# Self-attention of a transformer block: reciprocals two slots on between the maxima, second group transposed a slot later, values and projections a slot on, seven probability buffers

## The chip, the cores and the metric

The kernel runs on one core of one Trainium2 chip. The metric is the device time of one execution in microseconds (us); "before" is the median of three runs. A profile is one execution taken by the hardware profiler. In its rows PE is the matrix engine TensorE (PEld its weight loads), DVE is VectorE, ACT is ScalarE, POOL is GpSimd, and SP is the engine that issues nearly all of this kernel's DMAs. L504 is line 504 of the kernel.

## What is computed

One transformer block in float32 on x (2 x 1024 x 256) with a context (2 x 154 x 192): self-attention and cross-attention with 16 heads of 64, then a gated feed-forward layer of 1024. The reference, cut to its core:

```python
def _attention(xq, xkv, wq, wk, wv, wo, bo):
    q = (xq @ wq).reshape(B, S, N_HEADS, D_HEAD)
    k = (xkv @ wk).reshape(B, T, N_HEADS, D_HEAD)
    v = (xkv @ wv).reshape(B, T, N_HEADS, D_HEAD)
    attn = jnp.einsum('bihd,bjhd->bhij', q, k) * D_HEAD ** (-0.5)
    attn = jax.nn.softmax(attn, axis=-1)
    out = jnp.einsum('bhij,bjhd->bihd', attn, v).reshape(B, S, D_ATTN)
    return out @ wo + bo
h = _layernorm(x, ln1_g, ln1_b)
x = _attention(h, h, sa_wq, sa_wk, sa_wv, sa_wo, sa_bo) + x
h = _layernorm(x, ln2_g, ln2_b)
x = _attention(h, cond_emb, ca_wq, ca_wk, ca_wv, ca_wo, ca_bo) + x
h = _layernorm(x, ln3_g, ln3_b)
p = h @ ff_w1 + ff_b1
a, gate = (p[..., :D_FF], p[..., D_FF:])
return a * jax.nn.gelu(gate, approximate=False) @ ff_w2 + ff_b2 + x
```

## The kernel before

The order of all instructions is written out by hand (`tc.manual_schedule()`): each engine runs its own in the order in which the program issues them, and semaphores make it wait where data or a buffer isn't ready. What an engine has to do next is therefore stuck behind whatever it waits for.

**Units and slots.** A unit is a pair of heads of one batch (16 units). Self-attention has `SA` = 128 slots, eight per unit (`2 * SH`, `SH` = 4); in this text n is the slot's number within its unit, and a half is four slots, that is half of a unit's queries. A slot takes two groups of 64 queries for both heads. `LAG` is 2.

**One slot p, engine by engine.** PE computes the two groups' scores into two PSUM tiles `s` (`scores`, L493); with two such tiles, the first group of the next slot can only start when the exponentials have read the first tile, and the second likewise. The 1024 keys of a query are spread over two blocks of partitions, 512 each, so a row's softmax comes in two parts. DVE takes the negated maxima of a group over its part (L654), ACT the four exponentials with their sums (`exponents`, L504; two per group), into a probability tile `p` of which there are six buffers (`pp`). Then the two parts' maxima and sums, in the small tile `st`, are exchanged between partitions by four small DMAs on SP (`exchange`, L514). In the next slot `join` computes from them on POOL the differences `dd` (L522, L523), on ACT their exponentials `ee` (L525), on POOL `zz` and the denominators `den` (L527, L529). DVE takes the reciprocal `rd` (L600), and POOL scales the four probability parts by it (L604). One slot later DVE transposes both groups (`turn_groups`, L618) into `pT`, a tile for each half (two buffers). When the four slots of a half are all transposed, PE multiplies with the values in two parts (`self_values`, `weigh`, L539), and ACT copies the sum `po` to `o_sa` (L639).

**What fills PE beside scores and values.** Of the eight slots of a unit, four hold a part of `self_values` (n = 2, 3, 6, 7 before). In the other four `run_work` runs the next unit's projections `pq_sa`, `pk_sa` (L362) and `pv_sa` (L393), pieces of the output projection `py_sa` (L467, added to x by DVE at L474), transposes of a normalisation (`ph_ln`, L280) and products for cross-attention (`pk`, `pe`). The lists `work`, `side` and `outs` hold what is still to do. In the first half no values are ready, so its slots run projections.

**Order within a slot before:** scores and both maxima; four exponentials; `join` of slot p - 1; exchange of slot p; both transposes of slot p - 2; an addition to x if there is one; the reciprocal of slot p - 1 and its four scalings; POOL's addition of a bias from `later`; loads; PE's work. So on DVE the reciprocal of p - 1 is the last of slot p and stands ahead of the maxima of p + 1.

**SP's queue** holds the exchange of each slot, the weight loads of later units (`load_ahead`: queries at n = 2, keys at n = 3, values at n = 7), the swap of halves of `v_sa` (L409, L410, after the value projection), tiles of the second batch's x and chunks of `sa_wo` (`load_ahead_parts`).

**After slot 127** come 48 steps c of cross-attention (three per unit) that overlap with the last self-attention work, and then the feed-forward part.

Of the kernel before, what the change touches and what calls it, by code (L numbers as in the profile page):

```python
# [13 lines left out]
P = 128  # L14
# [4 lines left out]
def tile_transformer_block(ctx: ExitStack, tc: tile.TileContext, a: dict, out: bass.AP):  # L19
# [44 lines left out]
    pp_ = ctx.enter_context(tc.tile_pool(name="pp", bufs=6))  # L64
# [80 lines left out]
    def load_ahead_parts():  # L145

        wo["sa"] = const.tile([P, NPAIR, D], F32, tag="wo", name="sa_wo")  # L150
# [5 lines left out]
        def chunk(i):  # L156
            nc.sync.dma_start(out=wo["sa"][:, i, :], in_=w["sa_wo"][i * P:(i + 1) * P, :])

        tiles = [lambda t=t: tile_of_x(t) for t in tile_order("sa")]
        chunks = [lambda i=i: chunk(i) for i in range(NPAIR)]  # L160
# [300 lines left out]
    def out_piece(kind, b, g, t):  # L461
# [3 lines left out]
        for e in range(2):  # L465
            for i in range(HP):
                nc.tensor.matmul(  # L467
                    py[:, e * D:(e + 1) * D], lhsT=o[:, i, (t + e) * P:(t + e + 1) * P],
                    rhs=wo[kind][:, g * HP + i, :], start=(i == 0), stop=(i == HP - 1),
# [29 lines left out]

    def exponents(u, sc, st, i):  # L500
# [17 lines left out]
    def join(u, st):  # L518
# [4 lines left out]
        nc.gpsimd.tensor_scalar(dd, dd, 0.0, 1.0, op0=ALU.min, op1=ALU.mult)  # L523
        ee = small.tile([P, 2, 4], F32, tag="ee", name=f"ee_{u}")
# [24 lines left out]
    drain = []  # L549
# [42 lines left out]
    joins, groups, halves = [], [], {}  # L592

    def scale_groups(u, st, members):

        ee, den = join(u, st)

        def reciprocals():
            rd = small.tile([P, 4], F32, tag="rd", name=f"rd_{u}")
            nc.vector.reciprocal(rd, den)  # L600
            for i, pr in enumerate(members):
                for j in range(2):
                    c = 2 * i + j
                    nc.gpsimd.tensor_scalar(  # L604
                        pr[:, j, :], pr[:, j, :], rd[:, c:c + 1], ee[:, 0, c:c + 1],
                        op0=ALU.mult, op1=ALU.mult,
                    )
                groups.append(pr)

        return reciprocals  # L610

    def turn_groups(p):
        h, g = divmod(p, SH)
        if g == 0:
            halves[h] = pt_.tile([P, 2 * NK, QH // 2], F32, tag="pT", name=f"pT_{h}")
        for i in range(2):
            c = (2 * g + i) * KB
            nc.vector.transpose(  # L618
                halves[h][:, :, c:c + KB], groups.pop(0).rearrange("p j (n k) -> p (j n) k", k=KB)
            )  # L620
# [25 lines left out]
    def self_first(p):  # L646
# [6 lines left out]
        for i in range(2):  # L653
            nc.vector.tensor_reduce(st[:, 0, 0, i, :], sc[i], AX.X, ALU.max, negate=True)  # L654
# [32 lines left out]
    def load_ahead(p):  # L687
# [10 lines left out]
        if p == SA - 2:  # L698
            load_weights("ca", units[2][1], "q")
        if p == SH:  # L700
# [385 lines left out]
    with tc.manual_schedule():  # L1086
# [61 lines left out]
        for p in range(SA):  # L1148
# [7 lines left out]
            late = then()  # L1156
            if p >= LAG:
                turn_groups(p - LAG)
            if adds:
                adds.pop(0)()  # L1160
            if late:
                late()
            flush(kept)
            if later and (p < 4 or p % (2 * SH) in (2, 4, 6)):
# [4 lines left out]
            h, hg = divmod(p, SH)  # L1169
            if h == 0 or hg < LAG:  # L1170

                run_work(2 if p < SA - SH else 1, h % 2 or h == 0, sum_tile)
                if p == LAG:
                    load_weights("sa", units[1][1], "v")
                ui, n = divmod(p, 2 * SH)
# [163 lines left out]
```

## Time and profile before

| what | us |
|---|---|
| runs before | 1105.02, 1100.79, 1100.0; median 1100.79 |
| span of the profiled execution | 1100.3 |
| self-attention slots, first maxima of slot 0 to first cross scores | 18.8 to 713.4 |
| DVE's waits for `den` before the reciprocal (L600) | 34.9 in 43 waits |
| POOL's waits for the exchange before `dd` (L522) | 51.9 in 48 waits |
| ACT's waits for the maxima before the exponentials (L504) | 184.9 in 115 waits |

The profiled execution's own time is its span. A row of the timeline has the start in the span, the time of the merged instructions, engine, line, operation, tiles, count and, in brackets, the engine's idle time before it and what ended it. A row of the windows has the stretch, its length, the busy time of PE with the number of its instructions, TensorE's granted clock (1.00 is full), the DMA engines' share and GB/s. A row of the waits has the waiting engine and line, who ended the wait, total us, number and longest. A row of the DMA issues ends with the median time from issue to landing. Times of PE's matmuls overlap, and their ends are modelled, so starts are compared, not lengths.

### The profile page before, as it was taken

Reading aid. Unit: us, or ns where it says so; the run is one execution under the profiler, and the core shown is the slowest. Engines: PE = TensorE matmul, PEld = TensorE weight load, DVE = VectorE, ACT = ScalarE, POOL = GpSimd, SP = SyncE. Lnnn points to the kernel's source line nnn. Section 1 sums busy time; section 2 is a strip of 40 time slices with the busy share of each in tenths; the row PEclk is TensorE's granted clock in tenths of the full one; section 3 lists DMA queues with packets and bytes.
Section 4 is the critical chain, followed back from the end, with each engine's and each line's share of the span. In section 5 each row is a group of like instructions: output and inputs, shape, how many; then the busy total and the mean of one; then the engine's idle time right before and its main releaser. Section 6 shows DMA issues by size and latency. Waiting matters only on the chain.

```text
span 1100.3 us, 44912 instructions
## 1 busy us (share of the span) xinstructions
PE 1080.4 (98%) x18388; PEld 718.1 (65%) x18388; DVE 893.1 (81%) x1301; ACT 638.0 (58%) x2057; POOL 730.2 (66%) x1552
## 2 busy tenths in 40 slices
PE   8999999999999999999999999999999999899998
PEld 6556656556665565565665655567766677788887
DVE  5888999898989989999999989978877877644442
ACT  5666676667667656666776776666655554232221
POOL 2766777777777777677777777676756785555331
PEclk9999999999999999999999999999999999999999
DMA  3222112112111111111110111036765545000000
GB/s 93 67 61 52 45 40 57 39 46 52 25 42 43 29 42 32 39 42 24 42 42 14 42 33 28 20 82 159 179 155 123 117 106 114 1 10 10 15 15 29
DMA packets 104094, 60.71 MB, mean 55 GB/s; under 512 B 32330, under 2 KB 94674, under 8 KB 103890
## 3 DMA queue, kind: packets, MB, share of 16 engines
q1 hardware_dynamic: 102514, 57.07, 21.8%
q8 instruction: 145, 2.38, 0.9%
q10 hardware_dynamic: 1376, 0.79, 0.2%
q14 instruction: 59, 0.48, 0.1%
HBM read 27.91 MB, written 2.10 MB: 27 GB/s over the span
## 4 chain that ended last, share of the span: by engine, by line
PE 56%; ACT 12%; DVE 9%; DMA 8%; POOL 6%; SPq 5%; issue 4%; DVEq 0%; ACTq 0%; POOLq 0%
ACT p L504 11%; PE po L539 9%; PE s L493 9%; DVE st L654 6%; DMA st<-st 5%; PE pf L1069 5%; PE py_ca L467 5%; SPq L514 5%; PE poc L881 4%; PE pq_ca L362 4%; PE pb L1003 4%; PE py_sa L467 3%; PE sc L802 3%; PE pa L1003 2%; PE pc L1003 2%
## 5 line engine op out<-in xcount | busy, mean ns | idle before, releaser
L504 ACT ACTIVATE p<-s,st 128x512 f32<-128x512 f32 x512 | 345.3, 687 | 195.7 <-DVE st L654 184.9
L604 POOL TENSOR_SCALAR p<-p,rd,ee 128x512 f32<-128x512 f32 x512 | 385.7, 767 | 47.9 <-DVE rd L600 46.9
L654 DVE TENSOR_REDUCE st<-s 128x2 f32<-128x1024 f32 x256 | 300.7, 1216 | 23.7 <-PE s L493 9.4
L618 DVE STREAM_TRANSPOSE pT<-p 128x1024 f32<-128x1024 f32 x256 | 302.3, 1218 | 0.2 <-POOL p L604 0.2
L493 PE MATMUL s<-k_sa,q_sa 64*32 64x512 f32 x4096 | 261.0, 595 | 6.9 <-ACT p L504 6.0
L539 PE MATMUL po<-pT,v_sa 64*32 64x256 f32 x8192 | 239.8, 376 | 1.8 <-DVE pT L618 1.4
L539 PEld LDWEIGHTS po<-pT,v_sa 64*32 64x32 f32 x8192 | 174.9, 106 | 74.9 <-issue 22.0
L493 PEld LDWEIGHTS s<-k_sa,q_sa 64*32 64x32 f32 x4096 | 81.0, 106 | 111.6 <-ACT p L504 53.3
L818 ACT ACTIVATE p<-sc,neg 128x154 f32<-128x154 f32 x256 | 96.4, 407 | 82.9 <-DVE rden L826 79.7
L829 POOL TENSOR_SCALAR p<-p,rden 128x154 f32<-128x154 f32 x256 | 96.8, 398 | 56.9 <-DVE rden L826 56.5
L504 ACT ACTIVATION_READ_ACCUMULATOR p<-s,st 128x1 f32 x512 | 103.9, 203 | 0.0
L527 POOL TENSOR_TENSOR zz<-ee,st 128x8 f32<-128x8 f32 x128 | 25.9, 202 | 73.6 <-ACT ee L525 73.6
L393 PEld LDWEIGHTS pv_sa<-sa_wv,hT_ln 64*128 64x128 f32 x1024 | 58.5, 188 | 14.2 <-issue 7.5
L522 POOL TENSOR_TENSOR dd<-st 128x8 f32<-128x8 f32 x128 | 25.6, 200 | 55.5 <-DMA st<-st 51.9
L393 PE MATMUL pv_sa<-sa_wv,hT_ln 64*128 64x128 f32 x1024 | 61.7, 275 | 0.0
L467 PE MATMUL py_ca<-ca_wo,o_ca 128*128 128x256 f32 x256 | 60.0, 382 | 0.5 <-DVE o_ca L894 0.5
L467 PE MATMUL py_sa<-sa_wo,o_sa 128*128 128x256 f32 x256 | 59.7, 385 | 0.0
L467 PEld LDWEIGHTS py_sa<-sa_wo,o_sa 128*128 128x128 f32 x256 | 47.3, 190 | 17.8 <-ACT v_sa L402 6.7
L362 PE MATMUL pq_sa<-hT_ln,sa_wq 64*32 64x512 f32 (+1 forms) x976 | 58.8, 587 | 0.0
L362 PE MATMUL pq_ca<-hT_ln,ca_wq 64*128 64x512 f32 (+1 forms) x304 | 58.0, 589 | 0.0
L807 DVE TENSOR_REDUCE neg<-sc 128x6 f32<-128x924 f32 (+1 forms) x48 | 47.9, 999 | 12.1 <-PE sc L802 12.0
L362 PE MATMUL pk_sa<-hT_ln,sa_wk 64*32 64x512 f32 x960 | 57.4, 591 | 0.1
(117 smaller groups left out, 1462.9 us busy)
## 6 DMA issues: line engine op xcount, KB each, us to landing
wf<-pT_ca SPq DMA_DIRECT2D x128, 128.0 KB, 2.5
st<-st SPq DMA_DIRECT2D x512, 1.0 KB, 1.8
v_sa<-v_sa SPq DMA_DIRECT2D x32, 256.0 KB, 3.7
sa_wq<-in_L_xattn_sa_wq_dram SPq DMA_DIRECT2D x32, 128.0 KB, 3.2
sa_wk<-in_L_xattn_sa_wk_dram SPq DMA_DIRECT2D x32, 128.0 KB, 3.2
sa_wv<-in_L_xattn_sa_wv_dram SPq DMA_DIRECT2D x32, 128.0 KB, 3.0
ca_wq<-in_L_xattn_ca_wq_dram SPq DMA_DIRECT2D x32, 128.0 KB, 4.4
wf<-in_L_xattn_ff_w_dram SPq DMA_DIRECT2D x12, 256.0 KB, 3.9
```

What stands on the lines that cost most here:

```text
L362: nc.tensor.matmul(pq[r][f:f + m, at:at + n], lhsT=wt[own, c, f:f + m], rhs=h[own, c, t0:t0 + n], start=(c == 0), stop=(c == NH - 1), tile ...
L393: nc.tensor.matmul(pv[r][:, i * P:(i + 1) * P], lhsT=h[own, c, i * P:(i + 1) * P], rhs=wt[own, c, :], start=(c == 0), stop=(c == NH - 1), ...
L467: nc.tensor.matmul(py[:, e * D:(e + 1) * D], lhsT=o[:, i, (t + e) * P:(t + e + 1) * P], rhs=wo[kind][:, g * HP + i, :], start=(i == 0), st ...
L493: nc.tensor.matmul(sc[a4 * KB:(a4 + 1) * KB, j, :], lhsT=q[r, c:c + KB], rhs=k[r, h * HB:(h + 1) * HB], start=True, stop=True, tile_positi ...
L504: nc.scalar.activation(pr[:, j, :], sc[:, j, :], AF.Exp, bias=st[:, 0, 0, i, j:j + 1], accum_out=st[:, 0, 1, i, j:j + 1],)
L539: nc.tensor.matmul(po[a2][d:d + KB, :QH // 2], lhsT=v[r, t, e, d:d + KB], rhs=pT[r, d // DH * NK + n, :], start=(t == 0 and e == 0), stop= ...
L604: nc.gpsimd.tensor_scalar(pr[:, j, :], pr[:, j, :], rd[:, c:c + 1], ee[:, 0, c:c + 1], op0=ALU.mult, op1=ALU.mult,)
L618: nc.vector.transpose(halves[h][:, :, c:c + KB], groups.pop(0).rearrange("p j (n k) -> p (j n) k", k=KB))
L654: nc.vector.tensor_reduce(st[:, 0, 0, i, :], sc[i], AX.X, ALU.max, negate=True)
L818: nc.scalar.activation(pr_[:, j, i, :T], sc[:, j, i * T:(i + 1) * T], AF.Exp, bias=neg[:, j, i:i + 1], accum_out=den[:, j, i:i + 1],)
L829: nc.gpsimd.tensor_scalar(pr_[:, j, i, :T], pr_[:, j, i, :T], rden[:, j, i:i + 1], 1.0, op0=ALU.mult, op1=ALU.mult,)
L1003: nc.tensor.matmul(into[:, :BT], lhsT=lhs, rhs=wh[pair][i], start=first, stop=True, skip_group_check=True)
```

## The change

- The probability tiles get a seventh buffer. The room comes from the output weights: instead of one tile with all of `sa_wo` (later `ca_wo`), `load_out` loads the 256 KB for two head pairs into one of two buffers, again for each batch; for self-attention at n = 6 of every second unit, for cross-attention in the third step of every second unit.
- `join` is split into `differences` (`dd`) and `denominators` (`ee`, `zz`, `den`). POOL's order in slot p is now: two scalings of group 0 of p - 2, `dd` of p - 1, two scalings of group 1 of p - 2, `zz` and `den` of p - 1.
- The reciprocal of slot p - 2 stands between the two maxima of slot p.
- DVE then transposes group 1 of slot p - 3 and group 0 of slot p - 2.
- The values of a half start one slot later (n = 3, 4 and 7, 0), the other work moves to n = 1, 2, 5, 6, and in the first unit work runs in slots 0 to 6.
- The tail follows: the last half but one finishes its values in the first cross step, and the last reciprocals, scalings and transposes stand in cross steps 0 to 2.
- The tiles of the second batch's x are loaded in units 1 and 2.

```diff
-    pp_ = ctx.enter_context(tc.tile_pool(name="pp", bufs=6))
+    pp_ = ctx.enter_context(tc.tile_pool(name="pp", bufs=7))
...
-        pieces = tiles[:4] + chunks[:HP] + tiles[4:] + chunks[HP:]
-        slots = [u * 2 * SH + n for u in range(1, 5) for n in (0, 1, 4, 5)]
-        return dict(zip(slots, pieces))
+        slots = [u * 2 * SH + n for u in range(1, 3) for n in (0, 1, 4, 5)]
+        return dict(zip(slots, tiles))
+
+    def load_out(kind, b, g):
+
+        t = wo[kind, b, g] = p2.tile([P, HP, D], F32, tag="wo", name=f"{kind}_wo{b}_{g}")
+        c0 = g * HP * P
+        nc.sync.dma_start(
+            out=t, in_=w[f"{kind}_wo"][c0:c0 + HP * P, :].rearrange("(i p) d -> p i d", p=P))
...
+    def reciprocals(p):
+
+        v = slot[p]
+        v["rd"] = small.tile([P, 4], F32, tag="rd", name=f"rd_{p}")
+        nc.vector.reciprocal(v["rd"], v["den"])
+
+    def weighted(p, i):
+
+        v = slot[p]
+        pr = v["members"][i]
+        for j in range(2):
+            c = 2 * i + j
+            nc.gpsimd.tensor_scalar(
+                pr[:, j, :], pr[:, j, :], v["rd"][:, c:c + 1], v["ee"][:, 0, c:c + 1],
+                op0=ALU.mult, op1=ALU.mult,
+            )
...
+    def softmax_steps(p):
+
+        before, older = slot.get(p - 1), slot.get(p - 2)
+        if older:
+            weighted(p - 2, 0)
+        if before:
+            before["dd"] = differences(p - 1, before["st"])
+        if older:
+            weighted(p - 2, 1)
+
+    def softmax_join(p):
+
+        if p in slot:
+            v = slot[p]
+            v["ee"], v["den"] = denominators(p, v["st"], v["dd"])
...
-        for i in range(2):
-            nc.vector.tensor_reduce(st[:, 0, 0, i, :], sc[i], AX.X, ALU.max, negate=True)
+        maxima(sc[0], st, 0)
+        if p >= 2:
+            reciprocals(p - 2)
+        maxima(sc[1], st, 1)

         def then():
-            members = [exponents(f"{p}_{i}", sc[i], st, i) for i in range(2)]
-            late = scale_groups(*joins.pop(0)) if joins else None
+            members = [exponents(f"{p}_0", sc[0], st, 0)]
+            softmax_steps(p)
+            members.append(exponents(f"{p}_1", sc[1], st, 1))
+            softmax_join(p - 1)
             exchange(st)
-            joins.append((p, st, members))
-            return late
+            slot[p] = {"st": st, "members": members}
+            turn_group(p - 3, 1)
+            if p >= 2:
+                turn_group(p - 2, 0)
...
+        if n == 2 * SH - 2 and ui % HP == 1:
+            k = ui // HP
+            load_out("sa", *divmod(k, NQ))
...
-            if h == 0 or hg < LAG:
+            if p < 2 * SH - 1 or p % SH in (1, 2):

-                run_work(2 if p < SA - SH else 1, h % 2 or h == 0, sum_tile)
+                run_work(2 if p < SA - SH else 1, n > SH or p < SH, sum_tile)
...
             else:
-                run(lambda: self_values(h - 1, hg - LAG))
+                run(lambda: self_values(p // SH - 1 - (p % SH == 0), int(p % SH == 0)))
...
-            if c == 1:
-                turn_groups(SA - 2)
-            flush(drain)
+            if c < 2:
+                reciprocals(SA + c - 2)
             flush(lates)
+            if c < 3:
+                softmax_steps(SA + c)
+                if c == 0:
+                    softmax_join(SA - 1)
+                turn_group(SA + c - 3, 1)
+                if c < 2:
+                    turn_group(SA + c - 2, 0)
             lates.append(then())
...
-            if c == 1:
+            if c == 0:
+                run(lambda: self_values(2 * NU - 2, 1))
+            elif c == 1:
                 run(lambda: cross_queries(*nxt))
...
-                elif ui == HP:
-                    wo["ca"] = const.tile([P, NPAIR, D], F32, tag="wo", name="ca_wo")
-                    later[:0] = [lambda i=i: nc.sync.dma_start(
-                        out=wo["ca"][:, i, :], in_=w["ca_wo"][i * P:(i + 1) * P, :])
-                        for i in range(NPAIR)]
+                elif ui > HP and ui % HP == 1:
+                    load_out("ca", *divmod(ui // HP - 1, NQ))
...
+            if k == 0:
+                load_out("ca", B - 1, NQ - 1)
```

More of the change, by code (lines that the diff above doesn't have):

```diff
@@ L1155, in tile_transformer_block @@
             flush(stores)
-            late = then()
-            if p >= LAG:
-                turn_groups(p - LAG)
+            then()
             if adds:
                 adds.pop(0)()
-            if late:
-                late()
             flush(kept)
-            if later and (p < 4 or p % (2 * SH) in (2, 4, 6)):
+            ui, n = divmod(p, 2 * SH)
+            if later and (p < 4 or n in (2, 4, 6)):
                 later.pop(0)()
```

60 lines of the change are left out of this document (22 added, 38 removed).

## The prediction

> **What bounds the kernel now.** I read the page's busy shares first, then the time of whole head pairs on TensorE, then single slots engine by engine.
>
> ```profile
> PE 1080.4 (98%) x18388; PEld 718.1 (65%) x18388; DVE 893.1 (81%) x1301; ACT 638.0 (58%) x2057; POOL 730.2 (66%) x1552
> 60.25:671.29 611.04, 606.03 (x13748) 1.00 0.17 39
> 369.39:411.56 42.17, 42.17 (x985) 1.00 0.16 35
> 628.54:671.29 42.75, 42.75 (x988) 1.00 0.14 31
> L747 PE MATMUL pe<-ca_wv,ctxT 96*32 96x192 f32 (+1 forms) x48 | 2.4, 314 | 0.0
> 321.49 1.92 PE L493 MATMUL s<-k_sa,q_sa 64*32 64x512 f32 x32
> 323.21 3.66 PE L539 MATMUL po<-pT,v_sa 64*32 64x256 f32 x128
> 326.66 1.92 PE L493 MATMUL s<-k_sa,q_sa 64*32 64x512 f32 x32
> ```
>
> The three stretches begin where the scores of a unit's first slot begin: the first covers units 1 to 14, the others units 8 and 14, in which PE never stands; unit 14 has four normalisation transposes more, 0.58. In the last three rows a slot is 1.72 us of scores (321.49 to 323.21) and 3.45 of values (323.21 to 326.66): 5.17 us without a gap. So PE is the bound wherever it isn't held up, and the question is how often it is. Fourteen units at 42.17 are 590.4 us; the transposes, in eight of them by the program, add 4.6 and the products for `ends` 2.4. That makes 597.4 against 611.0: **PE loses 13.6 us in these 112 slots.** That is the ceiling for what the steady part of the change can give.
>
> Where it is lost shows in a slot with a late exchange, beside a quiet one:
>
> ```profile
> 333.34 2.35 DVE L654 TENSOR_REDUCE st<-s 128x2 f32<-128x1024 f32 x2
> 335.61 2.36 DVE L618 STREAM_TRANSPOSE pT<-p 128x1024 f32<-128x1024 f32 x2
> 338.08 0.18 DVE L600 RECIPROCAL rd<-den 128x4 f32<-128x4 f32 x1
> 338.38 1.23 DVE L654 TENSOR_REDUCE st<-s 128x2 f32<-128x1024 f32 x1
> 334.60 0.69 ACT L504 ACTIVATE p<-s,st 128x512 f32<-128x512 f32 x1 [1.18 <-DVE st L654]
> 337.27 0.22 ACT L525 ACTIVATE ee<-dd 128x8 f32<-128x8 f32 x1
> 333.32 3.01 POOL L604 TENSOR_SCALAR p<-p,rd,ee 128x512 f32<-128x512 f32 x4 [0.32 <-DVE rd L600]
> 336.30 0.20 POOL L522 TENSOR_TENSOR dd<-st 128x8 f32<-128x8 f32 x1
> 336.59 0.25 POOL L523 TENSOR_SCALAR dd<-dd 128x8 f32<-128x8 f32 x1
> 337.57 0.20 POOL L527 TENSOR_TENSOR zz<-ee,st 128x8 f32<-128x8 f32 x1 [0.73 <-ACT ee L525]
> 337.85 0.20 POOL L529 TENSOR_TENSOR den<-zz 128x4 f32<-128x4 f32 x1
> ```
>
> ```profile
> 204.62 2.35 DVE L654 TENSOR_REDUCE st<-s 128x2 f32<-128x1024 f32 x2
> 209.70 3.66 PE L539 MATMUL po<-pT,v_sa 64*32 64x256 f32 x128
> 213.64 1.09 PE L493 MATMUL s<-k_sa,q_sa 64*32 64x512 f32 x16 [0.27 <-ACT p L504]
> 216.00 3.84 PE L393 MATMUL pv_sa<-sa_wv,hT_ln 64*128 64x128 f32 x64
> 209.20 0.20 POOL L522 TENSOR_TENSOR dd<-st 128x8 f32<-128x8 f32 x1 [1.59 <-DMA st<-st]
> 210.57 0.18 DVE L600 RECIPROCAL rd<-den 128x4 f32<-128x4 f32 x1 [1.33 <-POOL den L529]
> DVE rd L600 <- POOL den L529: 34.9, 43, 3.1
> POOL dd L522 <- DMA st<-st: 51.9, 48, 13.9
> ```
>
> In the quiet slot the chain maxima, four exponentials, `ee`, `zz`, `den`, reciprocal fills 333.34 to 338.08, and the next maxima start at 338.38: 5.04 us, only 0.13 below PE's 5.17. DVE therefore pays back a delay at 0.13 us a slot. In the late slot `dd` waits for the exchange until 209.20, the reciprocal follows 1.37 later, and all of DVE has stood for 1.33. PE pays: values to scores take 3.94 instead of 3.45, and the scores 2.36 (213.64 to 216.00) instead of 1.72, 1.1 us together. The last two rows count such waits.
>
> **Part by part: the reciprocal.** It goes from the end of slot p+1 to between the maxima of slot p+2; 128 before and after, so no work is added. In time after a slot's first maximum, from the quiet slot: reciprocal at 1.14 (half of 333.34 to 335.61), the first two scalings 0.28 later (338.08 to 338.36 is the same step; the row at 333.32 is its predecessor) for 1.50 (half of 3.01), `dd` at 2.92 or when the exchange lands, 0.54 for its two operations, 1.50 for the other two scalings, 0.48 for `zz` and `den`: 5.44. Its reader stands at 5.17 + 1.14 = 6.31. So `dd` may start up to 3.75 before DVE is held; now it is 3.50 (5.17 less 0.30 less 1.37). But the second maximum now stands behind the reciprocal (0.18), so the second pair of exponentials, and with it the exchange, comes about 0.17 later. **The tolerance to a late exchange grows by 0.1 us only.** What is queued behind the waiting reciprocal is the second maximum and both transposes; for the maximum waits ACT's second pair, for that PE's next scores. What does improve is the pay-back:
>
> ```profile
> 317.55 2.36 DVE L654 TENSOR_REDUCE st<-s 128x2 f32<-128x1024 f32 x2 [1.35 <-DMA st<-st]
> 319.82 2.36 DVE L618 STREAM_TRANSPOSE pT<-p 128x1024 f32<-128x1024 f32 x2
> 322.11 0.66 DVE L474 TENSOR_TENSOR x<-py_sa,x 128x512 f32<-128x512 f32 x1
> 322.68 0.16 DVE L600 RECIPROCAL rd<-den 128x4 f32<-128x4 f32 x1
> 322.76 1.19 DVE L654 TENSOR_REDUCE st<-s 128x2 f32<-128x1024 f32 x1
> ```
>
> Where the reciprocal is ready, DVE's own slot is 2.27 + 2.29 + 0.08, or 4.64, up to 4.86 with a gap of 0.3 around the reciprocal: 0.3 to 0.5 us a slot against PE, not 0.13. The waits (43 in 128 slots) then mostly meet a DVE that has caught up. PE's slack for the second pair of exponentials: they end 3.93 after the maximum, at 326.69 in the slot of 322.76, and are needed at 326.66 + 0.86 = 327.52, so 0.83 now and 0.66 after. A stall of 1.33 less 0.1 less 0.66 leaves 0.57 of the 1.1 it costs now, and smaller ones less than that share. I take 8 of the 13.6 us as won. Bounds: 0 (tolerance all but unchanged, every wait still paid) and 13.6 (none paid).
>
> **Second transposition, scaling around `dd`, seventh buffer.** The second group's scaling ends at 4.96 and its transposition waits until the next slot: no wait. The first group's scaling ends at 2.92, its transposition stands at about 3.6: covered by 0.7; without it that much a slot. The exponentials reuse buffers whose transposition came a slot earlier, which needs seven; with six the second would wait inside its slot. Nothing, and POOL's bias additions now stand behind `den` and delay no `dd`: that is in the 8.
>
> **Values and projections a slot later.** Both move together, so each half's transposes still end a slot ahead of PE's use. But slot 6 has no large work for PE, since the first half's values begin in slot 7:
>
> ```profile
> 692.31:697.40 5.09, 3.38 (x52) 1.00 0.11 29
> 697.40:700.80 3.40, 3.40 (x33) 0.50 0.02 1
> 725.61 3.69 PE L539 MATMUL po<-pT,v_sa 64*32 64x256 f32 x128 [1.40 <-DVE pT L618]
> ```
>
> The 3.45 us of values that slot 6 has now move out of it. The next scores still wait for slot 6's exponentials: 1.27 from scores to maximum (321.49 to 322.76), 4.1 to the last exponential, 0.1 and 0.86 for the second group, 6.33 against 6.89 now. PE stands 3.45 - 0.56 = 2.9 us (2.4 to 3.45). The same happened once already: at 692.31 PE stood 1.7 of 5.09 us, and the clock was 0.50 for the next 3.40. I add 1.7 for that (0 to 3.4): **fill +4.6.** [...]
>
> At the end the moved half of values runs behind the first cross scores; it is the work that left slot 6, so only idle time counts. PE's wait of 1.40 for the last transpose becomes about 1.9, because that transpose now stands behind a slot's cross scalings on POOL: +0.5 (0 to 2.2, with a slow clock). The two slots without PE work near 695 get shorter by DVE's faster slot: -0.5 (0 to -0.9).
>
> **Loads.** Tiles of x come earlier; `sa_wo` and `ca_wo` come as 256 KB for each two head pairs, reloaded for each batch. On SP the self loads stand behind a slot's exchange, one in sixteen slots, eight slots ahead of their use, and the 16 chunks of 128 KB go. The halves of `v_sa` stand one slot later, still ahead of one exchange a unit. I take 0 (-1 to +2). The cross loads are a rival below.
>
> **Sum:** -8 + 4.6 + 0.5 - 0.5 = -3.4 on a span of 1100.3, so 1096.9; the median of the runs, 1100.79, lies 0.5 above the span: **1097.4**, within 0.5% (5.5 us, what counts here as no change).
>
> **Rivals.**
> (B) *All stalls paid back, clock kept at the fill.* -13.6 + 2.9 + 0.5 - 0.5 = -10.7: 1090.1. For it: the faster DVE, and unit 8 shows that 42.17 can be held. Against: the exchange's landing doesn't change.
> (C) *PE isn't the bound, and slots fall to the next loop.*
>
> ```profile
> 203.66 2.41 SPq L514 DMA_DIRECT2D st<-st  x4
> st<-st SPq DMA_DIRECT2D x512, 1.0 KB, 1.8
> ```
>
> A reciprocal depends on the one two slots before it: 0.16 to the second maximum, 2.6 to the end of its exponentials, 4.2 for the exchange (its four issues and a landing), 2.5 from `dd` to `den`; 9.5 for two slots, 4.75 for one, much like DVE's own 4.64 to 4.86. At 4.8 the 128 slots would take 0.37 less each beside the 10.7: 1043. [...] Against: PE's rows join without a gap at 5.17, and nothing in the diff shortens them.
> (D) *Slower: the exchange loop decides.* The threshold of `dd` has hardly moved, and a held reciprocal now delays the second exponentials, which have 0.66 of slack, not 0.83. From a `dd` start of about 3.6 us after the maximum (209.20 less 204.62, 4.58, in the late slot) each wait is paid as before and 0.17 more. None of the 13.6 is won, half of 43 waits cost 0.17 more (3.7), with fill and tail: +4.6 + 0.5 - 0.5 + 3.7 = +8.3, so 1109. Against: DVE's spare time.
> (E) *Cross attention waits for `ca_wo`*, so that the change doesn't do only what it says:
>
> ```profile
> 760.64 1.08 SPq L1256 DMA_DIRECT2D ca_wo<-in_L_xattn_ca_wo_dram  x2
> 768.14 1.89 PE L467 MATMUL py_ca<-ca_wo,o_ca 128*128 128x256 f32 x8
> wf<-in_L_xattn_ff_w_dram SPq DMA_DIRECT2D x12, 256.0 KB, 3.9
> ```
>
> A load of 256 KB takes 3.9, and some 7 us lie between issue and use. If SP is held 4 us, PE waits about 1 us for each of eight: -3.4 + 8 = +4.6, 1105.
>
> **Chances.** Forecast 0.46 (its own range 1093 to 1102), B 0.23, C 0.02, D 0.19, E 0.10. Faster by over 0.5% (below 1095.3): B, C and a quarter of the forecast, 0.36. Slower (above 1106.3): two thirds of D and a third of E, 0.16. The same: 0.48. The range 1088 to 1107 leaves out C, a fifth of B and over half of D, just under 0.2.
>
> **What would show it.** Right: DVE's waits before the reciprocal fall from 34.9 us to under 15 while those of `dd` on the exchange stay near 50; units 1 to 14 shrink by about 8 us to near 603; PE stands some 3 us behind the scores of slot 6 and the clock is 0.5 there; ACT's second pair starts later after the first. Wrong: a unit below 42 us (then PE wasn't the bound), reciprocal waits that stay, or PE waiting at the cross projections for `ca_wo`.

## The result and the profile after

The kernel after takes 1094.87 us (median of 9 runs, 1093.61 to 1099.67), the kernel before 1100.51 us (9 runs beside it, 1100.0 to 1105.02). The ratio is 0.9949, 95% interval 0.9936 to 0.9963: 5.6 us faster. The profiled execution after has a span of 1091.8 and took 1093.61; in all nine runs the time lies 1.8 us above the span.

First the page after: the busy shares, and the chain of work that ended last, by engine; the last row is that chain before.

```profile
PE 1070.7 (98%) x18388; PEld 703.4 (64%) x18388; DVE 881.2 (81%) x1301; ACT 643.5 (59%) x2057; POOL 729.9 (67%) x1552
PE 89%; DVE 3%; POOL 3%; ACT 2%; DMA 2%; SPq 1%; issue 1%; ACTq 0%; DVEq 0%; POOLq 0%
PE 56%; ACT 12%; DVE 9%; DMA 8%; POOL 6%; SPq 5%; issue 4%; DVEq 0%; ACTq 0%; POOLq 0%
```

The instruction counts are those of before. In the chain before, TensorE had 56%; the rest ran through ScalarE, VectorE, transfers and GpSimd. Now 89% of the chain is TensorE itself. Units 1 to 14, from the first scores of slot 8 to those of slot 120, and unit 14 alone, in the windows view after:

```profile
61.33:659.19 597.86, 597.80 (x13748) 354.37 (x13740) 547.43 (x625) 411.01 (x1203) 448.66 (x931) 1.00 0.18 42
616.45:659.19 42.74, 42.74 (x988) 24.89 (x980) 38.71 (x43) 29.18 (x89) 30.49 (x65) 1.00 0.15 33
```

611.04 us have become 597.86, with the same 13748 matmuls. The prediction worked out 597.4 for TensorE's own work there. The loss of 13.6 us has become 0.5. Unit 14, which had no gap before (42.75), is unchanged: TensorE is the bound now, and nothing in it became shorter. The waits (total us, times, longest):

```profile
POOL dd L526 <- DMA st<-st: 65.5, 62, 14.4
DVE rd L605 <- POOL den L537: 12.4, 19, 3.3
PE s L493 <- ACT p L508: 4.2, 6, 2.1
```

GpSimd waits for the exchange more often than before (62 times against 48). The exchanges came hardly earlier: in the mean of slots 8 to 121 `dd` starts 4.64 us behind the end of the exponentials, against 4.72 before. The reciprocal waits less (12.4 us against 34.9, 19 times against 43), and the waits that are left hardly reach TensorE. A late exchange in the timeline after: `dd` stands in slot 16, the reciprocal that needs it in slot 17 (start, duration, engine, instruction):

```profile
109.03 0.20 POOL L526 TENSOR_TENSOR dd<-st 128x8 f32<-128x8 f32 x1 [1.44 <-DMA st<-st]
109.55 1.52 POOL L613 TENSOR_SCALAR p<-p,rd,ee 128x512 f32<-128x512 f32 x2
109.82 1.23 DVE L502 TENSOR_REDUCE st<-s 128x2 f32<-128x1024 f32 x1 [0.47 <-ACT ee L533]
111.32 0.20 POOL L537 TENSOR_TENSOR den<-zz 128x4 f32<-128x4 f32 x1
111.56 0.18 DVE L605 RECIPROCAL rd<-den 128x4 f32<-128x4 f32 x1 [0.51 <-POOL den L537]
111.65 1.20 DVE L502 TENSOR_REDUCE st<-s 128x2 f32<-128x1024 f32 x1
112.88 0.69 ACT L508 ACTIVATE p<-s,st 128x512 f32<-128x512 f32 x1 [0.35 <-DVE st L502]
108.59 1.92 PE L493 MATMUL s<-k_sa,q_sa 64*32 64x512 f32 x32
110.31 3.64 PE L362 MATMUL pq_sa<-hT_ln,sa_wq 64*32 64x512 f32 x64
113.74 1.92 PE L493 MATMUL s<-k_sa,q_sa 64*32 64x512 f32 x32
```

`dd` starts 4.38 us after its slot's first maximum (104.65). That is nearly as late as in the late slot that the prediction showed (4.58), where VectorE stood 1.33 us and TensorE paid 1.1. Here the reciprocal waits 0.51, the second maximum with it, and ScalarE's second pair waits 0.35. TensorE's scores follow after 5.15 us (108.59 to 113.74) without a gap.

Where the time went, from the starts of the same instructions in both timelines:

| stretch | before | after | difference |
|---|---|---|---|
| first maximum of slot 0 to that of slot 8 | 44.19 | 43.66 | -0.53 |
| slot 8 to slot 120 (units 1 to 14) | 609.59 | 597.89 | -11.70 |
| slot 120 to slot 127 | 38.10 | 35.97 | -2.13 |
| slot 127 to the end of the last self values | 23.23 | 30.15 | +6.92 |
| to the first cross output projection | 34.25 | 34.52 | +0.27 |
| to the first product of the feed-forward's second weight | 201.45 | 200.01 | -1.44 |
| to the end | 130.69 | 130.70 | 0.01 |

The first and the fourth stretch belong together, since 3.45 us of values moved from the one to the other. The sum, with 0.11 at the start, is -8.49, while the medians differ by 5.6. The two profiled executions lie apart by chance as well: after's is 1.3 below the median of its kernel, and before's, if it too took 1.8 more than its span, is 1.6 above its own. The 1.44 seems to be chance of that kind; the last section returns to it.

The fill, in TensorE's timeline and in one window (the number behind the five engines is the granted clock):

```profile
50.16 1.95 PE L493 MATMUL s<-k_sa,q_sa 64*32 64x512 f32 x32
54.17 1.89 PE L493 MATMUL s<-k_sa,q_sa 64*32 64x512 f32 x16 [2.06 <-ACT p L508]
56.28 1.78 PE L493 MATMUL s<-k_sa,q_sa 64*32 64x512 f32 x16 [0.22 <-ACT p L508]
57.87 3.64 PE L547 MATMUL po<-pT,v_sa 64*32 64x256 f32 x128
54.34:57.75 3.41, 3.19 (x32) 0.47 (x26) 3.41 (x4) 1.54 (x5) 3.22 (x8) 0.50 0.87 216
```

Slot 6 has nothing but scores. TensorE stands 2.06 us and then runs 3.41 us at half clock. Slots 6 and 7 take 11.17 us (50.16 to 61.33) for 6.89 us of work (twice 1.72 of scores and 3.45 of values): 4.28 us above it.

The tail, in the timelines of TensorE and ScalarE:

```profile
710.98 0.79 PE L838 MATMUL sc<-kT,q_ca 64*128 64x154 f32 x8 [1.52 <-ACT p L854]
718.27 3.69 PE L547 MATMUL po<-pT,v_sa 64*32 64x256 f32 x128 [2.26 <-DVE pT L626]
708.50 0.21 ACT L533 ACTIVATE ee<-dd 128x8 f32<-128x8 f32 x1 [6.89 <-POOL dd L527]
708.61 0.37 ACT L854 ACTIVATE p<-sc,neg 128x154 f32<-128x154 f32 x1
```

`ee` of the last slot stands on ScalarE 6.89 us for the last exchange, and the first cross exponentials are queued behind it. That gives TensorE a wait of 1.52, and later one of 2.26 for the last transposes. Before, there was one of 1.40.

### The profile page after: what moved, and what is told of

The parts are those of the page before. It is cut to its first block, busy times and chain, and to the rows that moved or that the text cites. A ratio compares the mean times of both kernels' runs of the same rounds, so it can differ in the third digit from the quotient of the medians.

```text
span 1091.8 us, 44847 instructions
## 1 busy us (share of the span) xinstructions
PE 1070.7 (98%) x18388; PEld 703.4 (64%) x18388; DVE 881.2 (81%) x1301; ACT 643.5 (59%) x2057; POOL 729.9 (67%) x1552
## 4 chain that ended last, share of the span: by engine, by line
PE 89%; DVE 3%; POOL 3%; ACT 2%; DMA 2%; SPq 1%; issue 1%; ACTq 0%; DVEq 0%; POOLq 0%
PE s L493 19%; PE po L547 19%; PE py_sa L467 5%; PE pf L1105 5%; PE py_ca L467 5%; PE pv_sa L393 5%; PE pq_sa L362 5%; PE pk_sa L362 4%; PE poc L917 4%; PE pq_ca L362 4%; PE pb L1039 3%; PE sc L838 3%; PE pa L1039 2%; PE pc L1039 2%; PE ph_ln L280 1%; ACT p L508 1%
## 5 line engine op out<-in xcount | busy, mean ns | idle before, releaser
L613 POOL TENSOR_SCALAR p<-p,rd,ee 128x512 f32<-128x512 f32 x512 | 390.3, 773 | 98.1 <-DVE rd L605 93.7
L502 DVE TENSOR_REDUCE st<-s 128x2 f32<-128x1024 f32 x256 | 308.8, 1207 | 53.4 <-issue 16.8
L493 PE MATMUL s<-k_sa,q_sa 64*32 64x512 f32 x4096 | 252.0, 594 | 4.9 <-ACT p L508 4.2
L547 PE MATMUL po<-pT,v_sa 64*32 64x256 f32 x8192 | 235.8, 376 | 2.3 <-DVE pT L626 2.3
L547 PEld LDWEIGHTS po<-pT,v_sa 64*32 64x32 f32 x8192 | 169.2, 106 | 80.6 <-issue 27.1
L493 PEld LDWEIGHTS s<-k_sa,q_sa 64*32 64x32 f32 x4096 | 79.5, 106 | 106.6 <-issue 51.2
L526 POOL TENSOR_TENSOR dd<-st 128x8 f32<-128x8 f32 x128 | 25.8, 202 | 68.7 <-DMA st<-st 65.5
L843 DVE TENSOR_REDUCE neg<-sc 128x6 f32<-128x924 f32 (+1 forms) x48 | 48.0, 1000 | 13.2 <-PE sc L838 13.1
L854 ACT ACTIVATION_READ_ACCUMULATOR p<-sc,neg 128x1 f32 x256 | 57.1, 223 | 0.0
L362 PE MATMUL pq_sa<-hT_ln,sa_wq 64*32 64x512 f32 (+1 forms) x976 | 56.6, 586 | 0.0
```

The lines of the kernel that those rows point to most:

```text
L362: nc.tensor.matmul(pq[r][f:f + m, at:at + n], lhsT=wt[own, c, f:f + m], rhs=h[own, c, t0:t0 + n], start=(c == 0), stop=(c == NH - 1), tile ...
L493: nc.tensor.matmul(sc[a4 * KB:(a4 + 1) * KB, j, :], lhsT=q[r, c:c + KB], rhs=k[r, h * HB:(h + 1) * HB], start=True, stop=True, tile_positi ...
L502: nc.vector.tensor_reduce(st[:, 0, 0, i, :], sc, AX.X, ALU.max, negate=True)
L547: nc.tensor.matmul(po[a2][d:d + KB, :QH // 2], lhsT=v[r, t, e, d:d + KB], rhs=pT[r, d // DH * NK + n, :], start=(t == 0 and e == 0), stop= ...
L613: nc.gpsimd.tensor_scalar(pr[:, j, :], pr[:, j, :], v["rd"][:, c:c + 1], v["ee"][:, 0, c:c + 1], op0=ALU.mult, op1=ALU.mult,)
L854: nc.scalar.activation(pr_[:, j, i, :T], sc[:, j, i * T:(i + 1) * T], AF.Exp, bias=neg[:, j, i:i + 1], accum_out=den[:, j, i:i + 1],)
```

## The experiments

The first theory was the recorded one: the gain comes from the reciprocal's new place, which keeps VectorE from standing for late exchanges. The rivals: the loads, or the rest of the reordering. All ratios are to the kernel before, on the same chip; after's is 0.9949. Every kernel computes the whole reference.

### The loads alone

The kernel before, with the new loads of `wo` and `x` and nothing else:

```diff
+        if n == 2 * SH - 2 and ui % HP == 1:
+            k = ui // HP
+            load_out("sa", *divmod(k, NQ))
...
+                elif ui > HP and ui % HP == 1:
+                    load_out("ca", *divmod(ui // HP - 1, NQ))
```

> The kernel before with the new loads alone (wo in parts of 256 KB, the tiles of x earlier); order of the softmax, transposes and values as before. Theory 1 (the gain comes from the reciprocal's new place): 1100.5, within 2 us of before, and VectorE's waits of the reciprocal for den stay near 35 us. Rival 2 (the gain comes from the loads, which no longer delay exchanges): 1095 or less, and the waits of dd for the exchange fall below 45 us.

1101.72 us, ratio 1.0007 (0.9998 to 1.0016). Waits of the reciprocal 37.1 us, of `dd` 51.2: as before. The loads give nothing and cost nothing.

### The reciprocal back in its old place on VectorE

The kernel after, with the reciprocal of slot p at the end of slot p+1 again:

```diff
         maxima(sc[0], st, 0)
-        if p >= 2:
-            reciprocals(p - 2)
         maxima(sc[1], st, 1)
...
             if p >= 2:
                 turn_group(p - 2, 0)
+            if p >= 1:
+                reciprocals(p - 1)
```

> The kernel after with the reciprocal alone put back to the end of slot p+1, behind the transposes; scalings, transposes, values, loads and seven buffers as after. Theory 1: VectorE stands again for each late exchange, the waits for den come back to 30 us or more, and the 8 to 12 us of the steady part are lost: 1103 to 1107. Rival 3 (the gain comes from the rest: bias additions off the path of dd, scalings split around dd, the seventh buffer): 1095 to 1097.

1157.64 us, ratio 1.0503 (1.0484 to 1.0523): far worse than before itself, and far from both numbers expected. The waits:

```profile
DVE rd L605 <- POOL den L537: 97.3, 94, 4.2
PE s L493 <- ACT p L508: 34.3, 73, 3.7
```

The rest of the change does not bring the gain. Without the new place it does harm, because GpSimd now makes `den` behind the second pair of scalings: `dd` to `den` takes 2.61 us in the mean of slots 8 to 121, against 1.60 before.

### The reciprocal ahead of both maxima, and behind both

Two slots on as after, but not between the maxima:

```diff
+        if p >= 2:
+            reciprocals(p - 2)
         maxima(sc[0], st, 0)
-        if p >= 2:
-            reciprocals(p - 2)
         maxima(sc[1], st, 1)
```

> The kernel after with the reciprocal of slot p-2 ahead of both maxima of slot p, not between them. It is needed 1.14 us earlier in the slot. If its margin behind den is what counts (theory 1), about half of the gain goes: 1097 to 1101, waits for den 20 us or more. If only leaving the slot p+1 counts, not the place between the maxima: 1095 to 1096.

1149.01 us, ratio 1.0435 (1.0418 to 1.0452), waits for `den` 89.5 us. Both numbers expected were far off: standing one maximum (1.2 us) earlier in the slot doesn't cost half of the gain of 5.6, it costs 54 us against after. For the other side, `reciprocals(p - 2)` stands behind `maxima(sc[1], st, 1)`:

> The kernel after with the reciprocal of slot p-2 behind both maxima of slot p, not between them. dd may then start about 1.2 us later before VectorE is held (5.2 us behind the first maximum, not 4.07, the earliest that held it in the profile after). If margin against late exchanges is all that counts: waits for den near 0, and the few us of TensorE waits left in the steady part go, 1092 to 1094.9. Rival (the scalings now start so late that the transposes wait for them and dd stands behind the first scalings): 1097 or more, with waits of the transpose for p above 20 us.

1121.34 us, ratio 1.0193 (1.0179 to 1.0207). The waits:

```profile
DVE pT L626 <- POOL p L613: 71.0, 128, 2.8
DVE rd L605 <- POOL den L537: 3.2, 2, 3.0
```

The reciprocal no longer waits, but a transpose waits for its scaling in each of the 128 slots, and VectorE becomes the slower loop. The rival was right. The place between the maxima lies between two walls: earlier the reciprocal runs into `den`, later the transposes run into the scalings.

### Both transposes of a slot together

```diff
-            turn_group(p - 3, 1)
             if p >= 2:
                 turn_group(p - 2, 0)
+                turn_group(p - 2, 1)
```

> The kernel after with both transposes of slot p-2 in slot p, the second not a slot later. Its scalings end 4.96 us behind the first maximum by the prediction, so VectorE would stand for the second transpose in each slot. By that working: a slot of over 5.4 us instead of 5.17, 1110 or more, with waits of the transpose for p above 30 us. If the scalings are done in time all the same: within 2 us of 1094.9.

1226.26 us, ratio 1.1138 (1.1121 to 1.1155).

```profile
DVE pT L626 <- POOL p L613: 181.9, 256, 3.9
```

Every transpose waits. This is the cover that the prediction named for the later second transposition.

### Six probability buffers

```diff
-    pp_ = ctx.enter_context(tc.tile_pool(name="pp", bufs=7))
+    pp_ = ctx.enter_context(tc.tile_pool(name="pp", bufs=6))
```

> The kernel after with six probability buffers, not seven; all else as after. By the prediction's working the second pair of exponentials of slot p then waits for the second transposition of slot p-3, which stands behind both maxima of slot p: ACT's second pair starts about 3.7 us behind the first maximum instead of 2.6, past the 0.8 us that TensorE has to spare, and the loop of exponentials, exchange and dd grows from about 10.0 to 11.2 us for two slots: 0.2 to 0.4 us a slot, 1117 to 1140. If the seventh buffer does nothing: 1094 to 1096.

1145.85 us, ratio 1.0421 (1.0407 to 1.0435), a little above the 1117 to 1140 expected.

```profile
ACT p L508 <- DVE pT L626: 132.8, 106, 2.8
```

The exponentials wait for the transposition that is to free their buffer. The seventh buffer adds no speed by itself; without it the rest of the change is 51 us slower.

### A later exchange, in both kernels

One more transfer of 1 KB ahead of each exchange, in before and in after. It only shifts the exchange:

```diff
     def exchange(st):
 
+        for _ in range(1):
+            idle = small.tile([KB, 2, 2, 2], F32, tag="idle", name="idle")
+            nc.sync.dma_start(out=idle, in_=st[:KB, 0])
         for a4 in range(4):
```

> The kernel before with one more small transfer of 1 KB on SyncE, from the same maxima, ahead of each of the 128 exchanges: each exchange lands about 0.6 us later (a quarter of the four issues' 2.41 us), dd at a mean of 3.9 us behind the first maximum instead of 3.34, past the 3.50 that the prediction allows. Both theories: VectorE waits in nearly every slot and has 0.13 us a slot to make it good; 0.1 to 0.3 us more in each of 112 slots, 1112 to 1135, waits for den above 50 us.

> The kernel after with the same additional transfer of 1 KB ahead of each exchange. As the prediction had it (tolerance 3.75 instead of 3.50, every wait beyond it paid): dd near 4.0, 0.2 to 0.3 us a slot, 1110 or more. Rival (the wait now sits in a loop of two slots, 9.5 + 0.6 = 10.1 us, still shorter than TensorE's two slots of 10.34, and only moves VectorE behind TensorE without making TensorE wait): 1094 to 1099, although VectorE waits for den in most slots.

Before goes to 1138.71, ratio 1.0337 (1.032 to 1.0354), a little above what was expected; after to 1123.13, ratio 1.0193 (1.0174 to 1.0212). The waits, first before's kernel, then after's:

```profile
POOL dd L525 <- DMA st<-st: 111.3, 85, 14.6
DVE rd L603 <- POOL den L532: 73.5, 81, 3.8
PE s L493 <- ACT p L504: 23.3, 59, 1.7
```

```profile
POOL dd L529 <- DMA st<-st: 136.7, 96, 14.9
DVE rd L608 <- POOL den L540: 53.2, 55, 4.2
PE s L493 <- ACT p L508: 10.5, 18, 1.5
```

From the end of the exponentials to `dd` it takes 0.76 and 0.78 us longer (means 5.48 and 5.42 against 4.72 and 4.64). Before pays 3.4% for it, after 2.4%. So the new order has more room, but not enough for 0.8 us, and the rival's number (1094 to 1099) fell. Its mechanism, the loop of two slots, only had the wrong length: the 9.5 us of the prediction take 4.2 for the exchange, where 4.64 is measured after. Measured from the traces (means over slots 8 to 121, us after the first maximum or between the events), the loop runs: exponentials end, exchange, `dd` to the end of `den`, then 0.30 to the next first maximum where the reciprocal stands ahead of it or at the end of a slot. Where it stands behind the first maximum, that maximum's 1.23 is taken off instead.

| kernel | exponentials end | to `dd` | to `den` | reader | half of the sum | slot measured |
|---|---|---|---|---|---|---|
| before | 4.04 | 4.72 | 1.60 | +0.30 | 5.33 | 5.44 |
| after | 4.11 | 4.64 | 2.50 | -1.23 | 5.01 | 5.34 |
| before, exchange later | 4.04 | 5.48 | 1.44 | +0.30 | 5.63 | 5.73 |
| after, exchange later | 4.40 | 5.42 | 2.48 | -1.23 | 5.54 | 5.53 |
| six buffers | 5.48 | 4.55 | 2.54 | -1.23 | 5.67 | 5.73 |
| reciprocal at the end of a slot | 4.04 | 4.53 | 2.61 | +0.30 | 5.74 | 5.85 |
| reciprocal ahead of both maxima | 4.04 | 4.57 | 2.57 | +0.30 | 5.74 | 5.77 |

TensorE's own slot is 597.4 / 112 = 5.33. Six of the seven lie within 0.11 of half the loop. The kernel after lies at TensorE's slot, the only one with half a loop clearly below it. Before, the loop and TensorE were equal in the mean, which leaves no room for an exchange later than the mean. The sums are read from each kernel's own trace: they show how little slack the loop has, and are no forecast. Worked out ahead, with the 5.48 put into the row before and the 5.42 and the +0.30 into the row after, they would have been 5.71, 5.40 and 5.78, against 5.73, 5.53, and 5.77 and 5.85. The kernels in which the transposes wait for their scalings are not in the table, since another wait decides there.

### Filling slot 6

The three products for the cross keys 3 to 5 move from slots 14 to 16 into the hole:

```diff
+                if p == 2 * SH - 2:
+                    for i in range(3):
+                        run(lambda: context_keys(3 + i, mm_tile if i else sum_tile))
...
-                if n == SH + 2 and ui in (1, NU - 1):
+                if n == SH + 2 and ui == NU - 1:
```

> The kernel after with the three products for the cross keys 3 to 5 in slot 6 instead of slots 14 to 16 (3.6 us of TensorE in the stretch where it stood 2.3 us and then ran 3.4 us at clock 0.50). If the prediction's fill term is right: the gap is filled and the clock stays at 1.0 there, 2.6 to 4.0 us less, 1090.9 to 1092.3. Rival (the time is lost to another engine there, or the keys' weights come too late): 1094 to 1096. If a gap of about 2 us doesn't lower the clock but something else did, the half clock stays and only 2.3 go: 1092.6.

1095.67 us, ratio 0.9945 (0.9931 to 0.9958): no gain, as the rival's number had it, but for another reason. TensorE's timeline:

```profile
52.19 3.50 PE L762 MATMUL pk<-ctxT,ca_wk 96*128 96x320 f32 x12
55.62 1.95 PE L493 MATMUL s<-k_sa,q_sa 64*32 64x512 f32 x32
92.83 1.95 PE L493 MATMUL s<-k_sa,q_sa 64*32 64x512 f32 x32
96.84 1.09 PE L493 MATMUL s<-k_sa,q_sa 64*32 64x512 f32 x16 [2.06 <-ACT p L508]
```

The hole is filled and the clock stays at 1.0 (1.00 from 50 to 62). But slot 14 has lost what filled it and now has the hole of 2.06 us. The second try takes nothing from a later slot: the value projection of the second head pair in two pieces, in slots 5 and 6.

```diff
-        return [costing(2, q), costing(2, k)] + value_pieces(b, pr, 1)
+        return [costing(2, q), costing(2, k)] + value_pieces(b, pr, 2 if (b, pr) == units[1] else 1)
```

> The kernel after with the value projection of the second head pair in two pieces, in slots 5 and 6, not in slot 5 alone, so that no slot stands empty of large work and no slot further on loses its filler. If the hole in slot 6 and its half clock cost what the profile after shows (4.2 us above TensorE's own work in the slots 0 to 7 there): slots 5 and 6 take about 5 us each, 1 to 3 us less in all, 1092 to 1094. Rival (two half-full slots are held by VectorE and ScalarE and lose as much together): 1094.5 to 1096.

1096.39 us, ratio 0.9967 (0.9956 to 0.9979). The rival's number nearly fits, but its reason does not. Slots 5 and 6 do take 4.6 us each (44.61 to 53.79 for both), and the first maximum of slot 8 comes 1.9 us earlier than after's. By slot 24 it is 0.1. SyncE's queue, GpSimd and VectorE show where most of the time goes:

```profile
57.72 1.60 SPq L134 DMA_DIRECT2D sa_wk<-in_L_xattn_sa_wk_dram  x2
59.84 0.62 SPq L409 DMA_DIRECT2D v_sa<-v_sa  x1
60.52 0.63 SPq L410 DMA_DIRECT2D v_sa<-v_sa  x1
61.31 3.23 SPq L518 DMA_DIRECT2D st<-st  x4
```

```profile
66.35 0.20 POOL L526 TENSOR_TENSOR dd<-st 128x8 f32<-128x8 f32 x1 [1.60 <-DMA st<-st]
68.87 0.18 DVE L605 RECIPROCAL rd<-den 128x4 f32<-128x4 f32 x1 [1.24 <-POOL den L537]
```

Slot 7's exponentials end at 59.66. Its exchange is issued 1.7 us later, behind the copies of `v_sa`, and `dd` starts 6.7 us after the exponentials instead of 4.64. The reciprocals in slots 8 and 9 wait 1.04 and 1.24 us, and slots 8 and 10 run 0.4 and 0.6 us over TensorE's work; the rest goes in smaller pieces up to slot 22. Without the hole, the queue of loads that falls into the same slots comes to the surface.

### The tail

Cross exponentials ahead of the last `ee` on ScalarE, and the last self scalings ahead of the first cross scalings on GpSimd:

```diff
-            flush(lates)
             if c < 3:
                 softmax_steps(SA + c)
+            flush(lates)
+            lates.append(then())
+            if c < 3:
                 if c == 0:
                     softmax_join(SA - 1)
...
-            lates.append(then())
```

> The kernel after with two moves behind the last slot: cross exponentials of slot c go to ScalarE ahead of ee of slot 127, and the last self scalings go to GpSimd ahead of the first cross scalings. If the 1.5 and 2.3 us that TensorE waits there come from these two orders: 1.5 to 3 us less, 1091.9 to 1093.4. Rival (the last transposes are late because of the last exchange itself): same as after, 1094 to 1096.

1093.65 us, ratio 0.9925 (0.9911 to 0.9939), the fastest measured here; 2.6 us below after by the ratios, though the two intervals touch. TensorE's timeline and ScalarE's:

```profile
712.30 0.69 PE L838 MATMUL sc<-kT,q_ca 64*128 64x154 f32 x8
719.12 3.69 PE L547 MATMUL po<-pT,v_sa 64*32 64x256 f32 x128 [1.76 <-DVE pT L626]
712.08 0.21 ACT L533 ACTIVATE ee<-dd 128x8 f32<-128x8 f32 x1 [4.11 <-POOL dd L527]
```

The wait of 1.52 is gone. From slot 127's first maximum to the end of the values it is 27.99 us instead of 30.15. The wait for the transposes shrank only from 2.26 to 1.76: here the last exchange itself is late, as the rival had it.

### Two queues for the exchange

With the tail's moves, and two of the four transfers issued by ScalarE:

```diff
-            nc.sync.dma_start(
+            (nc.sync if a4 < 2 else nc.scalar).dma_start(
...
-            softmax_join(p - 1)
             exchange(st)
+            softmax_join(p - 1)
```

> The kernel after with the two moves of e9_tail at the end, and with two of an exchange's four transfers issued by ScalarE right behind the second exponentials, the other two by SyncE as before (2.41 us of issues in a row become about 1.2 beside each other). If late exchanges still set what TensorE loses in the steady part and behind the fill: dd starts about 0.5 to 1.2 us earlier behind the exponentials (4.64 us in the mean now), the waits for den go from 7.9 us to under 2, and 1 to 4 us go beside the tail's 1 to 2: 1089 to 1092. Rival (ScalarE pays for the issues, about 1.2 us a slot, and its second exponentials come later than the 0.8 us that TensorE has to spare): 1097 or more.

1109.73 us, ratio 1.0075 (1.0057 to 1.0092). The waits, and ScalarE's queue in one slot:

```profile
POOL dd L526 <- DMA st<-st: 21.3, 15, 13.8
PE pk_sa L362 <- ACT q_sa L377: 5.8, 15, 1.1
DVE rd L605 <- POOL den L537: 5.4, 12, 0.7
333.29 1.17 ACTq L518 DMA_DIRECT2D st<-st  x2
```

The exchange is hardly waited for now: `dd` starts 0.3 us earlier behind the exponentials than in the kernel with the tail alone (4.38 against 4.71). But ScalarE's `ee` comes behind the issues, and `dd` to `den` takes 3.20 instead of 2.48. TensorE loses more than it did: the 1.17 us of issues stand ahead of the copies of a projection's result, and the next projection waits for them once in each unit. That slot takes 0.4 to 1.3 us more than in the kernel after, 8.6 us over units 1 to 14, which take 15.9 more in all; 5.8 of the rest fall into the slot of the value projection, and what it waits for is not shown here. The rival's number was right, and so was the cost of the issues on ScalarE; it is paid at these copies.

## Why the prediction was right or wrong

**TensorE as the bound, and the ceiling of 13.6 us:** right. Units 1 to 14 stand at 597.86 against 597.4 worked out, and unit 14 did not change. Rival C fell with it.

**"The tolerance to a late exchange grows by 0.1 us only":** wrong, and the step that failed. In slots 8 to 121 the earliest `dd` behind which the reciprocal has a wait on record started 3.48 us after its slot's first maximum before and 4.07 after. A wait of 0.50 belongs to a `dd` at 3.75 before, one of 0.51 to a `dd` at 4.38 after: VectorE stands 0.6 us less for the same lateness. Three terms were off. The 3.50 for before is where TensorE's slot begins to grow; VectorE's instructions ahead of the reciprocal end at 4.63 there, so with 1.37 from `dd` it stands from 3.26 on. The maximum that the reciprocal now follows takes 1.22, not 1.14, so in slots of 5.17 the reader stands at 6.39, not at 6.31. And the second exponentials were to come 0.17 later. In quiet slots they do not, because ScalarE's first pair ends behind the second maximum anyway; their end moved from 4.04 to 4.11 in the mean. The working of `dd` to `den` was right (2.52 against 2.50). The loops of the table say the same: 0.9 us longer to `den`, a reader 1.53 us later, 0.6 us of room for two slots. So 18 exchanges of 114 lay beyond 4.0 after, where 36 had lain beyond 3.5 before.

**8 us won:** mis-sized for that reason: with 0.6 in place of 0.1 the prediction's own sum leaves 0.07 of the late slot's stall to TensorE, not 0.57. It was 13.2 in the windows of the two profiled executions, nearly the steady term of rival B. Other executions agree roughly: the same 112 slots take 610.81 with the new loads alone, and 598.69 in the kernel after with only the tail moved. The waits that are left cost TensorE nothing, as in slot 17, where 0.51 on VectorE became 0.35 on ScalarE and none on TensorE.

**Rival D, the loop of the exchange:** it did not decide, because its loop is 10.0 us for two slots, under TensorE's 10.66. But the mechanism is real. With an exchange 0.78 later it does decide, at 5.54 a slot, and 0.6 us of slack for the exchange is what the change has gained.

**Second transposition, scaling around `dd`, seventh buffer at nothing:** right as a price in the whole, and each cover is worth much: 131 us without the one, 51 without the other, against after. That GpSimd's bias additions now stand behind `den` was not tried alone.

**Fill +4.6:** 4.28 measured in slots 6 and 7. The mechanism was right and the two sizes were off against each other: the gap was 2.28 (2.06 and 0.22), shorter than the 2.9 and under its range, and the half clock cost the other 2.0, not 1.7. Whether the kernel is slower by it is another matter. Both ways of filling the hole removed it and gained nothing, the one by a new hole, the other by late exchanges.

**Tail +0.5:** mis-sized. The stretch grew by 6.92 - 3.45 = 3.5, of which TensorE's two waits make 3.78 - 1.40 = 2.4. What was overlooked is ScalarE's queue: the cross exponentials stand behind an `ee` that waits for the last exchange. Moving them gave 2.16 back.

**The two slots near 695 at -0.5:** -2.1 from slot 120 to 127, without the half clock that stood there before (0.50 from 697.38 to 700.79).

**Loads at 0:** right, 1.0007. Rival E fell: TensorE waits nowhere for `ca_wo`.

**Median 0.5 over the span:** wrong. A run takes 1.8 more than its own span, and the profiled execution of before was a long one. Taken from its median, before's usual span is 1098.7.

**The sum of -3.4:** it stands against -8.49 between the two executions. The steady part won 5.2 more, slots 120 to 127 1.6 more, the feed-forward 1.4 that nobody had forecast, and the fill cost 0.2 less (4.4 up to the scores of slot 8); the tail cost 3.0 more and smaller pieces 0.4. The medians differ by 5.6; the other 2.9 are the chance of these two executions. So it is in part luck that 1097.4 lies only 2.5 above the median of 1094.87: misses of opposite sign made up for each other, and the 0.51% stand at the edge of the 0.5% that the prediction called no change. Two of its signs came as said (waits before the reciprocal of 12.4, the half clock behind slot 6). Two did not: units 1 to 14 went to 597.9, not near 603, and the waits for the exchange to 65.5, not near 50.

## What to carry to other kernels

When a step with a late input is moved in an in-order queue, write down the loop that its input comes from, over as many slots as it spans, and compare half or a third of it with the bound's own slot, in means and not for the quiet slot. Here this sum, read from the traces, lay within 0.11 us of the slot in the six kernels that it held, and TensorE's own slot told the seventh. The best place lies between two walls, the input's arrival and the readers' need, and being one 1.2 us instruction off cost 26 us on one side and 54 on the other. A hole in the bounding engine may be covering a queue that is late at that place, so filling it is worth what a run shows, not its length.

## What the runs showed of the hardware

In the traces of the kernels before and after the half-clock stretches of TensorE, but for the one at the end of the span, are 3.41 us long (0.50 from 697.38 to 700.79 before, from 54.34 to 57.75 after) or 6.83 (0.50 from 960.20 to 967.03 before). After the gap of 2.06 us in slot 6 the clock fell in the kernel after, and so it did after the 2.08 in slot 6 of the kernel with the tail moved (0.50 from 55.70 to 59.11). After the same gap of 2.06 us at 94.8 in the kernel with slot 6 filled it stayed at 1.0 (1.00 from 92.83 to 104), and so it did behind the wait of 2.26 at 718 after:

```profile
718.27:721.70 3.43, 3.43 (x128) 2.50 (x128) 3.27 (x6) 2.60 (x11) 2.45 (x9) 1.00 0.02 5
```

Some 9 us ahead of the first product of the feed-forward's second weight (969.59) it fell for 6.83 us in before's execution, but not in after's (1.00 from 957 to 968) and not in the one with the loads alone (1.00 from 950 to 968). There lies more than the 1.44 of the table of stretches: six pairs of products in a row start 0.85 us apart in before's half clock, 0.43 apart behind it, 2.5 us in all. So in these executions the length of a gap did not decide by itself.

In the same two traces the stretches at full clock are 202, 76 and 39 times 3.413 us long before (689.50, 259.41 and 133.12) and 14 and 303 times after (47.79 and 1034.24). Cut into pieces of 3.413 us from the start of each, these are the pieces in which TensorE stood longest, but for the last at the end of each span:

| kernel | piece | TensorE stood | clock in the next piece |
|---|---|---|---|
| after | 50.93 to 54.34 | 2.06 | 0.50 |
| before | 956.79 to 960.20 | 1.75 | 0.50 |
| after | 716.52 to 719.93 | 1.75 | 1.00 |
| after | 952.04 to 955.45 | 1.73 | 1.00 |
| before | 693.96 to 697.38 | 1.71 | 0.50 |

In the others it stood 1.29 us or less, and the clock stayed at 1.00. After's gap of 2.06 in slot 6 lies whole in one piece, and the wait of 2.26 at 718 is split over two, with 0.52 and 1.75. These five are all that the two traces show; between 1.71 and 1.75 it went both ways.
